# A first stage planned anew: a longer written list of steps, tile 0's root first, clamps moved off GpSimd, more tiles turned by DMA

## The chip, the cores and the metric

The kernel runs on one core of a Trainium2 chip. The metric is the device time of one execution in microseconds (us); the time of a kernel is the median of its runs. The engines are named as the profile names them: PE (TensorE), with PEld for its weight loads, DVE (VectorE), ACT (ScalarE), POOL (GpSimd) and SP (SyncE, which here only issues DMAs).

## The reference

Two graph layers, each after a layer normalisation and with a residual, over 3327 nodes of 1024 features, all in float32:

```python
# layer 0
h = jnp.maximum(_layernorm(x), 0.0)
x = x + _L0_gnn_ref(h, adj, ...)
# layer 1
h = jnp.maximum(_layernorm(x), 0.0)
x = x + _L1_gnn_ref(h, adj, ...)
```

The first layer is quantised. Its first part, which the first stage of the kernel computes, is

```python
w_norm = (weight - mean) / std
weight_q = _weight_quant(w_norm, wgt_alpha, 3)     # clip to +-1, round to 7 steps, keep the sign
x = _act_quant(input, act_alpha, 4)                # min(x / alpha, 1), round to 15 steps
support = relu(jnp.matmul(x / act_delta, weight_q / wgt_delta) * act_delta * wgt_delta)
support_q = _act_quant(support, act_alpha2, 4)
output = jnp.matmul(adj / adj_scaling_factor, support_q / support_delta)
```

so it turns 3327 x 1024 rows into small integers, multiplies them by a 1024 x 1024 matrix of small integers, and clips and rounds the result again. The product with the adjacency matrix is the second stage; the attention of the second layer and a chain of four dense layers follow.

## The kernel before

The nodes are cut into T = 26 tiles of 128 rows. The first stage makes s_int[t], one 128 x 1024 tile of integers for each t, and they stay in SBUF for the second stage.

*The weights.* The 1024 x 1024 matrix w is loaded by SP as 8 blocks of 128 rows (L347), behind the two halves of x's tile 0 (L345) and ahead of tiles 1 to 5 (L128). Mean and deviation of the weights come from statistics of each block: blocks 0 and 3 on ACT (`measure_on_scalar`, L252 to L257, a sum and a sum of squares), the other six on DVE (L364). They are joined by two small matmuls (L412, L419). Then each half block (c, k), of 128 x 512, is rounded to a byte (`round_weight`: ACT L448 or DVE L446) and clamped to +-7 into w_int (`clamp_weight`: POOL or DVE, L452). There are 16 half blocks; three of the clamps and six of the roundings are on DVE.

*One tile of rows.* A tile t passes through these steps:

- `half_stats` (bn_stats, L234, two halves) and `aggregate` (L241) on DVE give mean and variance.
- `normaliser` gives scale and bias of a pair of tiles: eps added (L271), a square root on ACT (L273), two reciprocals on DVE (L275, L280), and small arithmetic (L277, L278, L282 to L284) on POOL, or on DVE where it is given `nc.vector`. Tiles 0 and 1 have chains of their own: `half_inverse` (L133 to L136) with `scale_and_bias` (L368, L369), and the steps `first_0` to `first_3`.
- `to_bytes` (ACT, L293) normalises and rounds to bytes; `quantise` (L301, the step `clip`) clamps them to 15 as bf16 in xq, which has three buffers. They are shared with the scratch output (`junk`) of the weight statistics on ACT.
- The tile is turned so that features lie on partitions, into xqt (four buffers). Either PE does it (`transpose`, L311, eight transposes of 128 x 128, and `transposed`, ACT L314, which copies the PSUM result), or a DMA from SP (L305). `by_tensor(t)` says which: before, PE for t up to 6 and for even t.
- `products(t, c)` (L321): 8 matmuls for each of 2 column halves, accumulated in PSUM (three buffers).
- `support_bytes` (ACT, L336, the step `sum`) rounds to bytes, `support` (L339) clamps them into s_int[t].

*The order.* Nearly every instruction of the stage is pinned: each engine executes its instructions in the order in which the program writes them. The start of the stage is written out as a list of steps, the string ORDER. A step `round_0_2_v` rounds half block (0, 2) on DVE, `product_0_1_3_3` is tile 0, column half 1, k from 3 to 3, and `bytes_3` also issues the load of the pair of tiles 8 and 9. The list goes as far as the last product of tile 4. From there a loop over t takes over. Its iteration for t does, in this order: part of the normaliser of pair t // 2 + 2 (for even t), the statistics of tile t + 6, the rest of that normaliser, support of tile t - 1, bytes and clip of tile t + 3 with the load of a pair ahead of the clip, the first half of tile t's products, the turn of tile t + 2 where PE does it, and the second half. The iteration for t = 5 takes two tiles of statistics, and turns tile t + 1:

```python
            for t in range(5, T):
                ...
                if t == 5:
                    steps = normaliser(4, V)
                ...
                for u in (10, 11) if t == 5 else (t + 6,):
                ...
                ahead = t + 1 if t == 5 else t + 2
```

*The second stage* (L680) multiplies the transposed adjacency, split into a high and a low part, by s_int. Its first part is made from a load (L170) that the same loop places at t = T - 2; on SP's queue that load stands behind the last turn by DMA.

Of the kernel before, what the change touches and what calls it, by code (L numbers as in the profile page):

```python
# [8 lines left out]
F32 = mybir.dt.float32  # L9
# [6 lines left out]
ALU = mybir.AluOpType  # L16
# [4 lines left out]
P = 128  # L21
# [24 lines left out]
GT = 2  # L46
# [14 lines left out]
def two_layer_kernel(  # L61
# [101 lines left out]
    with tc.tile_pool(name="at", bufs=2, reuse_waits="tile") as atp:  # L163
# [35 lines left out]
        with tc.tile_pool(name="s1", bufs=2, reuse_waits="tile") as s1, tc.tile_pool(  # L199
# [95 lines left out]
            def by_tensor(t):  # L295
                return t % 2 == 0 or t < 7
# [10 lines left out]
            def transpose(t):  # L307
                tps[t] = tp_ps.tile([P, KF, P], BF16, name="tp")
                xq = xqs.pop(t)
                for k in range(KF):  # L310
                    pin(nc.tensor.transpose(tps[t][:, k, :], xq[:, k * P : (k + 1) * P], ident_b))  # L311
# [72 lines left out]
            next(by_act[0])  # L384
            ready[0] = scale_and_bias(half_inverse(mv0[:, 1:2], "x0", pin), mv0[:, 0:1], to_q, "x0")
            next(by_act[0])
            to_bytes(0)
            quantise(0, nc.gpsimd)
            transpose(0)
            weight_statistics(1)  # L390
# [38 lines left out]
            v1, s1_, r1, q1, b1_ = (small.tile([P, 1], F32, name=f"x1{c}", bufs=1) for c in "vsrqb")  # L429
# [24 lines left out]
            def first(i):  # L454

                if i == 0:
                    pin(nc.vector.reciprocal(r1, s1_))
                elif i == 1:
                    pin(nc.gpsimd.tensor_tensor(q1, v1, r1, ALU.mult))
                    pin(nc.gpsimd.tensor_tensor(q1, q1, s1_, ALU.add))  # L460
                elif i == 2:
                    pin(nc.vector.reciprocal(r1, q1))
                else:
                    pin(nc.gpsimd.tensor_scalar(r1, r1, to_q, -1.0, ALU.mult, ALU.mult))
                    pin(nc.gpsimd.tensor_tensor(b1_, mv1[:, 0:1], r1, ALU.mult))
                    pin(nc.gpsimd.tensor_scalar(r1, r1, -1.0, None, ALU.mult))
                    ready[1] = r1, b1_
# [8 lines left out]
            def bytes_of(t):  # L476
# [7 lines left out]
                first_0 round_0_0 round_0_2_v first_1 round_0_5_v clamp_0_2 round_0_1 first_2 clamp_0_5  # L484
                clamp_0_0_v round_0_3 round_0_6_v product_0_0_0_0 first_3 round_0_4 stats_2_0 clamp_0_1
                bytes_1 stats_3_0 clamp_0_3 product_0_0_1_2 stats_2_1 clamp_0_4 product_0_0_3_3 round_0_7
                clip_1 clamp_0_6 product_0_0_4_5 round_1_0 stats_3_1 turn_1 clamp_0_7_v product_0_0_6_6
                round_1_1 clamp_1_0 mv_2 product_0_0_7_7 mv_3 turned_1 clamp_1_1 norm_1 round_1_2_v
                round_1_5_v clamp_1_2 norm_1 product_1_0_0_0 round_1_3 product_1_0_1_1 norm_1
                product_1_0_2_2 clamp_1_5 norm_1 product_1_0_3_4 round_1_4 norm_1 product_1_0_5_5 clamp_1_3  # L490
                norm_1 product_1_0_6_6 round_1_6_v product_1_0_7_7 round_1_7 product_0_1_0_0 clamp_1_4
                product_0_1_1_2 stats_4_0 bytes_2 product_0_1_3_3 clamp_1_6 product_0_1_4_5 clamp_1_7_v
                product_0_1_6_6 stats_5_0 product_0_1_7_7 product_1_1_0_0 bytes_3 product_1_1_1_1 clip_2
                product_1_1_2_4 stats_4_1 product_1_1_5_5 sum_0 turn_2 stats_5_1 product_1_1_6_7 clip_3
                turned_2 support_0 mv_4 turn_3 mv_5 sum_1 norm_2 product_2_0_0_0 stats_6_0 product_2_0_1_3
                stats_7_0 product_2_0_4_4 norm_2 product_2_0_5_5 turned_3 product_2_0_6_6 norm_2
                product_2_0_7_7 support_1 norm_2 product_2_1_0_1 norm_2 product_2_1_2_2 norm_2
                product_2_1_3_4 stats_6_1 bytes_4 product_2_1_5_7 stats_7_1 product_3_0_0_2 mv_6 bytes_5
                product_3_0_3_3 clip_4 product_3_0_4_6 mv_7 product_3_0_7_7 product_3_1_0_0 norm_3 sum_2
                clip_5 product_3_1_1_1 turn_4 stats_8_0 product_3_1_2_3 turned_4 support_2 product_3_1_4_4  # L500
                stats_9_0 product_3_1_5_7 norm_3 stats_8_1 product_4_0_0_0 sum_3 product_4_0_1_2 norm_3
                product_4_0_3_3 norm_3 product_4_0_4_5 norm_3 product_4_0_6_6 norm_3 product_4_0_7_7
                product_4_1_0_0 support_3 stats_9_1 product_4_1_1_1 bytes_6 turn_5 mv_8 product_4_1_2_2 mv_9
                product_4_1_3_4 turned_5 product_4_1_5_6 clip_6 product_4_1_7_7 bytes_7 clip_7
# [4 lines left out]
            for step in ORDER:  # L509
# [10 lines left out]
                elif op == "support":  # L520
# [5 lines left out]
                    support(*at, nc.gpsimd)  # L526
# [12 lines left out]
            for t in range(5, T):  # L539
# [4 lines left out]
                if t == 5:  # L544
                    steps = normaliser(4, V)
                elif t % GT == 0 and pair < T // GT:
                    steps = normaliser(pair)
                for _ in range(4):
                    next(steps, None)
                for u in (10, 11) if t == 5 else (t + 6,):  # L550
                    if u < T:
                        measure(u)
# [10 lines left out]
                ahead = t + 1 if t == 5 else t + 2  # L563
                if ahead < T and by_tensor(ahead):
                    transpose(ahead)
                    transposed(ahead)
# [553 lines left out]
```

## Time and profile before

| | |
|---|---|
| median of three runs | 2250.61 us (2249.75 to 2250.79) |
| the profiled execution's own time | 2246.05 us |
| its span | 2244.1 us |
| first product of the first stage (L321) | starts at 24.41 us |
| first product of the second stage (L680) | starts at 136.12 us |
| clamps of s_int on POOL / on DVE (L339) | 4 of 2.78 us / 22 of 0.70 us |
| copies of turned tiles on ACT (L314) | 16 of 1.01 us |
| turns by DMA (L305) | 10, issue 1.23 us each |

The profile is of one execution, whose own time lies 4.6 us below the median. Times in the trace are counted from the start of its span. In a timeline a row has the start, the duration, the engine, the line and the operands, the number of instructions that it merges, and in brackets the idle time ahead of it with what ended it.

### The profile page before, as it was taken

How to read it: one execution, taken by the hardware profiler on the slowest of the kernel's cores; microseconds unless marked ns; L12 is line 12 of the kernel's file. 1: busy time of each engine (PE TensorE's matmuls, PEld its weight loads, DVE VectorE, ACT ScalarE, POOL GpSimd, SP SyncE). 2: the span in 40 equal slices, each digit the busy share in tenths (PEclk: the TensorE clock that was granted, in tenths of full speed). 3: DMA queues.
4: the chain of work that ended last, by engine and by line, in shares of the span. 5: the costliest groups of instructions: out<-in, count | busy, mean ns of one | idle time of the engine just before them, and what ended most of it. 6: DMA issues, size and time to landing. Idle time of an engine off the chain costs nothing.

```text
span 2244.1 us, 31348 instructions
## 1 busy us (share of the span) xinstructions
PE 2190.6 (98%) x12512; PEld 1747.5 (78%) x12512; DVE 1534.3 (68%) x1983; ACT 1120.3 (50%) x1690; POOL 195.2 (9%) x284
## 2 busy tenths in 40 slices
PE   4999999999999999899999999999999999999998
PEld 2467777777777777699999999999999999744444
DVE  7744555555555545578999999999999999822211
ACT  6744445544454444456556555565655555531120
POOL 4300111110111101100000000000000000000000
PEclk9999999999999999999999999999999999999999
DMA  5654666555665566844242241655242422383311
GB/s 190 163 173 144 188 179 182 157 162 174 182 180 160 153 180 182 289 156 147 78 143 86 80 132 45 224 173 155 86 147 77 144 88 78 99 208 105 111 56 56
DMA packets 236978, 320.63 MB, mean 143 GB/s; under 512 B 99796, under 2 KB 180644, under 8 KB 236832
## 3 DMA queue, kind: packets, MB, share of 16 engines
q1 hardware_dynamic: 216280, 245.45, 36.2%
q0 software_dynamic: 20544, 73.18, 10.4%
q8 instruction: 98, 1.61, 0.3%
q14 instruction: 48, 0.39, 0.1%
q10 hardware_dynamic: 8, 0.00, 0.0%
HBM read 209.25 MB, written 86.79 MB: 132 GB/s over the span
## 4 chain that ended last, share of the span: by engine, by line
PE 53%; ACT 1%; DVE 0%; DMA 0%; issue 0%; DVEq 0%
PE acc L993 27%; PE mps L786 13%; PE o L1064 8%; PE h_ps L1027 4%; ACT enct L1049 0%; PE h_ps L949 0%; DMA weights<-in_w1t 0%; ACT h L1034 0%; DVE sel L984 0%; DVE nodes L1060 0%; ACT su L830 0%; DVE su L827 0%; DVE yo L1074 0%; ACT rest L957 0%; DVEq L1117 0%
## 5 line engine op out<-in xcount | busy, mean ns | idle before, releaser
L984 DVE SCALAR_TENSOR_TENSOR sel<-srow,ndst,mask 128x896 fp32r<-128x896 f32 (+1 forms) x832 | 864.4, 1079 | 51.1 <-PE acc L993 46.0
L786 PE MATMUL mps<-dw,mf 128*128 128x260 f32 x2704 | 452.6, 283 | 0.1
L680 PE MATMUL mm<-s_int,hi 128*128 128x512 f32 x1352 | 427.2, 397 | 0.0
L680 PE MATMUL mm<-s_int,lo 128*128 128x512 f32 x1352 | 419.2, 391 | 0.0
L993 PE MATMUL acc<-f_even,sel 128*128 128x260 f32 x2704 | 398.4, 285 | 6.8 <-issue 5.1
L993 PE MATMUL acc<-f_odd,sel 128*128 128x260 f32 x2704 | 393.8, 286 | 1.0 <-ACT xs L1008 1.0
L785 ACT CAST mf<-mask 128x1664 fp32r<-128x1664 uint8 x208 | 331.5, 1594 | 112.7 <-PE mps L786 94.9
L786 PEld LDWEIGHTS mps<-dw,mf 128*128 128x128 f32 x2704 | 377.2, 188 | 0.5 <-ACT part L790 0.3
L993 PEld LDWEIGHTS acc<-f_even,sel 128*128 128x128 f32 x2704 | 355.7, 189 | 11.8 <-issue 5.9
L993 PEld LDWEIGHTS acc<-f_odd,sel 128*128 128x128 f32 x2704 | 352.6, 188 | 8.4 <-issue 2.9
L680 PEld LDWEIGHTS mm<-s_int,hi 128*128 128x128 f32 x1352 | 253.9, 188 | 63.6 <-issue 12.0
L680 PEld LDWEIGHTS mm<-s_int,lo 128*128 128x128 f32 x1352 | 252.0, 188 | 51.5
L179 DVE TENSOR_SCALAR mk<-at 128x896 uint8<-128x896 f32 (+1 forms) x104 | 61.5, 593 | 227.3 <-DMA at<-in_adj_t 227.1
L614 PE MATMUL whm<-whead,ht 128*128 128x512 f32 x416 | 184.3, 596 | 5.6 <-ACT ht L591 5.3
L1064 PE MATMUL o<-weights,h 128*128 128x512 f32 x416 | 179.7, 592 | 0.0
L1064 PEld LDWEIGHTS o<-weights,h 128*128 128x128 f32 x416 | 79.1, 190 | 99.1 <-issue 98.8
L174 ACT CAST hi<-at 128x896 fp32r<-128x896 f32 x104 | 92.5, 890 | 125.5 <-PE mm L680 85.0
L614 PEld LDWEIGHTS whm<-whead,ht 128*128 128x128 f32 x416 | 77.7, 190 | 99.2 <-issue 87.1
L855 POOL DMA_DIRECT2D enc_d<-eh x64 | 57.5, 903 | 935.0 <-ACT eh L853 875.4
L790 ACT COPY part<-mps 128x260 f32<-128x260 f32 x104 | 39.2, 377 | 194.2 <-PE mps L786 194.2
L178 DVE TENSOR_TENSOR lo<-at,hi 128x896 fp32r<-128x896 f32 x104 | 106.0, 1020 | 41.3 <-ACT hi L174 41.1
L1034 ACT ACTIVATE h<-h_ps,rest 128x512 f32<-128x512 f32 (+1 forms) x54 | 35.1, 654 | 196.1 <-PE h_ps L1027 196.1
(166 smaller groups left out, 1700.9 us busy)
## 6 DMA issues: line engine op xcount, KB each, us to landing
feat_d<-fw POOLq DMA_DIRECT2D x26, 1040.0 KB, 5.3
f_even<-feat_d SPq DMA_DIRECT2D x7, 3380.0 KB, 13.3
f_odd<-feat_d SPq DMA_DIRECT2D x7, 3380.0 KB, 12.9
at<-in_adj_t SPq DMA_DIRECT2D x52, 448.0 KB, 3.9
at<-in_adj_t SPq DMA_DIRECT2D x52, 384.0 KB, 3.6
mask<-mask_d SPq DMA_DIRECT2D x39, 416.0 KB, 7.8
dw<-dsum_d SPq DMA_DIRECT2D x16, 910.0 KB, 8.8
dsum_d<-dw POOLq DMA_DIRECT2D x26, 520.0 KB, 6.3
```

Of the source, the lines that this page charges most:

```text
L174: ins = nc.scalar.copy(hi, at)
L178: nc.vector.tensor_tensor(lo, at, hi.bitcast(F32), ALU.subtract)
L179: ins = nc.vector.tensor_scalar(mk[:, r], at, 0.0, None, ALU.is_gt)
L614: ins = nc.tensor.matmul(whm, ht[:, k, :], whead[:, k, :], start=(k == 0), stop=(k == KF - 1))
L680: nc.tensor.matmul(mm[:, c * 512 : (c + 1) * 512], which[:, q, :], s_int[j][:, c * 512 : (c + 1) * 512], start=(j == 0 and which is hi), s ...
L785: nc.scalar.copy(mf, mask[:, j : j + TH, :])
L786: nc.tensor.matmul(ps, mf[:, j % TH, :], dw[:, j, :], start=(j == 0), stop=(j == T - 1))
L855: nc.gpsimd.dma_start(enc_d[q, sub[0] * P : (sub[-1] + 1) * P, h * HD : (h + 1) * HD].rearrange("(b p) d -> p b d", p=P), eh[:, q].rearran ...
L984: nc.vector.scalar_tensor_tensor(sel[:, :nb], srow[:, :nb], ndst[:, j, h : h + 1], mask[:, :, j, :], ALU.is_gt, ALU.mult,)
L993: nc.tensor.matmul(accs[b], sel[:, b, :], f[:, j, :], start=(j == 0), stop=(j == T - 1))
L1027: nc.tensor.matmul(ps[:, :cols], wt[:, k, m * P : (m + 1) * P], xt[:, k, :cols], start=(k == 0), stop=(k == k_n - 1),)
L1064: nc.tensor.matmul(ps[:, c * 512 : (c + 1) * 512], h3[:, k, q * P : (q + 1) * P], w4[:, k, c * 512 : (c + 1) * 512], start=(k == 0), stop= ...
```

## The change

Five edits, all in the first stage. `by_tensor` names fewer tiles: 0 to 4 without gaps, then every third, where before it was 0 to 6 and then every second. The square root chain of tile 0 comes ahead of the sums of weight block 0 on ACT. Tile 1's root is computed on DVE instead of POOL (one fused multiply-add and `scale_and_bias` in place of five POOL instructions). The early supports go to DVE like all others. And ORDER is a new list that goes three tiles further, through the last product of tile 7 with everything that must be under way by then, so that the loop starts at t = 8 and the special cases for t = 5 fall away.

```diff
             def by_tensor(t):
-                return t % 2 == 0 or t < 7
+                return t % 3 == 0 or t in (1, 2, 4)
...
-            next(by_act[0])
             ready[0] = scale_and_bias(half_inverse(mv0[:, 1:2], "x0", pin), mv0[:, 0:1], to_q, "x0")
-            next(by_act[0])
             to_bytes(0)
             quantise(0, nc.gpsimd)
             transpose(0)
+            for _ in range(2):
+                next(by_act[0])
             weight_statistics(1)
...
                 elif i == 1:
-                    pin(nc.gpsimd.tensor_tensor(q1, v1, r1, ALU.mult))
-                    pin(nc.gpsimd.tensor_tensor(q1, q1, s1_, ALU.add))
+                    pin(nc.vector.scalar_tensor_tensor(q1, v1, r1, s1_, ALU.mult, ALU.add))
                 elif i == 2:
                     pin(nc.vector.reciprocal(r1, q1))
                 else:
-                    pin(nc.gpsimd.tensor_scalar(r1, r1, to_q, -1.0, ALU.mult, ALU.mult))
-                    pin(nc.gpsimd.tensor_tensor(b1_, mv1[:, 0:1], r1, ALU.mult))
-                    pin(nc.gpsimd.tensor_scalar(r1, r1, -1.0, None, ALU.mult))
-                    ready[1] = r1, b1_
+                    ready[1] = scale_and_bias(r1, mv1[:, 0:1], to_q, "x1")
...
             ORDER = """
-                first_0 round_0_0 round_0_2_v first_1 round_0_5_v clamp_0_2 round_0_1 first_2 clamp_0_5
-                clamp_0_0_v round_0_3 round_0_6_v product_0_0_0_0 first_3 round_0_4 stats_2_0 clamp_0_1
-                bytes_1 stats_3_0 clamp_0_3 product_0_0_1_2 stats_2_1 clamp_0_4 product_0_0_3_3 round_0_7
...
-                product_4_1_3_4 turned_5 product_4_1_5_6 clip_6 product_4_1_7_7 bytes_7 clip_7
+                first_0 round_0_1 first_1 first_2 first_3 round_0_0 clamp_0_1 round_0_2_v round_0_5_v
+                bytes_1 clamp_0_2 clamp_0_0_v clamp_0_5 round_0_6_v product_0_0_0_1 round_0_3
...
+                turned_4 product_3_1_4_4 stats_9_0 product_3_1_5_7 norm_3 support_0 product_4_0_0_3 norm_3
+                sum_3 product_4_0_4_4 norm_3 product_4_0_5_6 norm_3 norm_3 product_4_0_7_7 product_4_1_0_1
+                stats_8_1 bytes_6 product_4_1_2_3 stats_9_1 product_4_1_4_6 mv_8 bytes_7 product_4_1_7_7
+                clip_6 product_5_0_0_1 mv_9 product_5_0_2_2 norm_4 product_5_0_3_3 clip_7 product_5_0_4_4
...
+                norm_5 product_7_1_3_4 clip_9 bytes_10 product_7_1_5_7 support_4 turn_9 turned_9 clip_10
+                stats_12_0 stats_13_0 stats_12_1 stats_13_1 mv_12 mv_13 support_5 support_6
             """.split()
...
-                    support(*at, nc.gpsimd)
+                    support(*at)
...
-            for t in range(5, T):
+            for t in range(8, T):
...
-                if t == 5:
-                    steps = normaliser(4, V)
-                elif t % GT == 0 and pair < T // GT:
+                if t % GT == 0 and pair < T // GT:
                     steps = normaliser(pair)
...
-                for u in (10, 11) if t == 5 else (t + 6,):
-                    if u < T:
-                        measure(u)
+                if t + 6 < T:
+                    measure(t + 6)
...
-                ahead = t + 1 if t == 5 else t + 2
-                if ahead < T and by_tensor(ahead):
-                    transpose(ahead)
-                    transposed(ahead)
+                if t + 2 < T and by_tensor(t + 2):
+                    transpose(t + 2)
+                    transposed(t + 2)
```

In the new list 13 of the 16 weight clamps stay on POOL, and three (half blocks 0_0, 0_7 and 1_7) are on DVE. Beside them POOL keeps, in this stage, the clip of tile 0, a few one-column constants, and from pair 6 on the small arithmetic of the normaliser.

## The prediction

> **What bounds the kernel now.** I read the page's engine shares and slices first. TensorE (PE) is busy for 98% of the span and in every slice at nine tenths or more except the first, at four. The change touches only the first stage, so the question is what PE waits for there.
>
> ```profile
> PE 2190.6 (98%) x12512; PEld 1747.5 (78%) x12512; DVE 1534.3 (68%) x1983; ACT 1120.3 (50%) x1690; POOL 195.2 (9%) x284
> PE   4999999999999999899999999999999999999998
> ```
>
> Next the timeline of PE over the first 140 us: start, duration, work, and in brackets the idle time before it with its releaser.
>
> ```profile
> 24.41 0.58 PE L321 MATMUL mm<-w_int,xqt 128*128 128x512 bf16 x1 [3.03 <-ACT wb L448]
> 27.26 1.44 PE L321 MATMUL mm<-w_int,xqt 128*128 128x512 bf16 x3 [2.27 <-POOL w_int L452]
> ...
> 53.27 1.90 PE L321 MATMUL mm<-w_int,xqt 128*128 128x512 bf16 x8 [1.24 <-ACT xqt L314]
> ...
> 61.79 3.32 PE L321 MATMUL mm<-w_int,xqt 128*128 128x512 bf16 x8 [4.44 <-ACT xqt L314]
> 64.95 0.61 PE L311 MATMUL tp<-ident_b,xq 128*128 128x128 bf16 x8
> 65.39 7.07 PE L321 MATMUL mm<-w_int,xqt 128*128 128x512 bf16 x32
> ```
>
> The first product starts at 24.41. From 61.79 on PE never stops: the second stage's first product (L680) follows at 136.12. So whatever the first stage saves moves everything after it. Between 24.41 and the stage's last matmul end (136.47) lie 112.1 us. Its work is 416 products at 0.2158 (32 take 7.07, 8 take 1.89) = 89.8, and 15 tiles turned by PE at 0.44 (64.95 to 65.39) = 6.6. The other 15.7 us are waits (10.9 in the timeline's brackets) and matmuls at half pace. The longest wait is explained by the timelines of ScalarE (ACT) and VectorE (DVE):
>
> ```profile
> 55.31 1.10 ACT L336 ACTIVATE sb<-mm,to_s 128x1024 uint8<-128x1024 f32 x1
> 59.60 1.24 ACT L293 ACTIVATE xb<-xs,l0b,l0r 128x1024 uint8<-128x1024 f32 x1 [3.19 <-issue]
> 60.74 0.99 ACT L314 COPY xqt<-tp 128x1024 bf16<-128x1024 bf16 x1
> ```
>
> ```profile
> 57.35 1.23 DVE L234 BATCH_NORM_STATS2 stats<-xs 128x6 f32<-128x512 f32 x2
> ...
> 59.15 0.16 DVE L283 TENSOR_TENSOR l0b<-mv,l0r 128x2 f32<-128x2 f32 x1
> ```
>
> Tile 6 was turned by 55.6, but its copy out of PSUM (60.74) stands on ACT behind the bytes of tile 8, whose scale DVE finishes at 59.5, after four statistics of tiles 10 and 11. It is a fault of order at the seam where the written list ends and the loop begins (t = 5), not of load.
>
> **What the Trainium skill says.** "TensorE: Matmul & The Clock Gate", Part 1 (What's actually happening): after an idle window of about 3.4 us PE runs at half clock until it has been busy for such a window, and the window is free-running. The trace agrees: after 4.44 idle, 8 products take 3.32 instead of 1.89, and the granted clock in the stretch 60 to 70 is 0.83. Since the window is free-running, another execution need not pay this 1.4 to 1.7 us. "GPSIMD Engine Reference", 1. Specifications: GpSimd (POOL) shares its SBUF interfaces with DVE. The trace agrees: beside POOL's 2.8 us clamps the tiny scale of L284 takes up to 0.89 on DVE, alone 0.17. "DMA: Bandwidth & Descriptors", DMA Transpose (X-bar), has the plain transpose only from the Sync and Scalar queues, so the new ones share SP's queue with the row loads; here all ten run on SP, and their times to landing are:
>
> ```profile
> DMA to landing us min/median/max: 3.0/5.3/5.6
> ```
>
> Those issued within a microsecond of a pair of row loads landed after 5.1 to 5.6, two without loads ahead after 3.0.
>
> **The change part by part.** I walked both lists instruction by instruction: each starts when its engine is free, its inputs are there and its buffer is free, with durations and spacings from the groups above and handoffs of 0.03 to 0.09 us read off the timelines. For the kernel before, this gives the first product at 24.46 (trace 24.41), the long wait as 4.62 (4.44) and the stage's end at 136.02 (136.47), so I trust it to about half a microsecond where the same mechanisms rule. For the changed list it gives 24.29 and 126.29. By parts:
>
> *First root first.* x0's square root no longer stands behind the first weight block's sum on ACT, which waits until 7.6 for its load; one of two table loads (1.28) goes, since the root's table is now loaded first. Tile 0's bytes start at 7.6 instead of 11.74, POOL clips them by 11.7 instead of 16.17. DVE can begin the weight statistics when block 1 lands instead of at 11.62. But weights land one per 1.28 us (7.6, 8.9, 10.2 and so on; the loads' times to landing of 5.9 to 9.0 and the row loads waiting for them show it), block 7 at about 16.6. So the weights' mean starts at 17.9 instead of 19.15: 1.25 gained, not 4. Block 3's sum on ACT now waits for xq's buffer until PE has turned tile 0 (12.65); it ends at 15.4, ahead of 17.9, and costs nothing.
>
> *Tile 1's root on DVE.* Five tiny instructions (0.16 to 0.22 each, dependent) stand ahead of DVE's first weight rounding: about 1.0. Three POOL waits and five POOL instructions (0.19 to 0.38) go, so POOL starts its weight clamps at 22.5 instead of 23.9. All 13 clamps stay on POOL at 0.775 apart, three on DVE. Product 0 of column 1, k = 6, the last that a POOL clamp holds up, starts at 33.88 instead of 35.59: **-1.7**. By then 22 products are done in both lists, so 394 remain in both.
>
> *Fewer turns by PE.* 12 tiles instead of 16 (0 to 4, 6, 9 and so on by 3): 4 x 8 transposes off PE, 4 x 0.44 = **-1.8**, and four copies of 0.9 off ACT. Each becomes an issue of 1.23 us on SP's queue, behind the row loads (0.33 to 0.45 each). SP is idle most of the stage; its next customer is the adjacency load, which still follows the last transpose (116.6 instead of 126.57) and so stays some 4 us ahead of its use.
>
> *The seam moved from t = 5 to t = 8, the list planned anew.* POOL's four support clamps (2.78 each) and three more tiles' go to DVE at 0.63: 4 x 0.63 = 2.5 us more on DVE, which has 6.0 us idle between 35 and 62 in the walk of before, and no POOL work stretches its tiny instructions there. In the new walk DVE idles 5.1 there, but only 0.4 of 14 us between 62 and 76, where its supports meet the loop's first statistics. PE's waits after 34 become 0.72 (tile 5, the first turned by DMA), 0.16 (tile 8), 1.29 (the turn of tile 12, behind DVE's clip) and 0.84 (tile 11): 3.0. Before, they were 1.11 + 0.38 + 1.24 + 4.44 = 7.2, with 0.17 of pipeline end at each, and 1.6 of half clock: 9.5. **-6.5**.
>
> Sum: -1.7 - 1.8 - 6.5 = **-10.0**, or -9.7 walk against walk. Against the profiled execution's own 2246.05 that is 2236. The median of the runs, 2250.61, lies 4.6 higher; I take the difference as holding for it, less 0.8 for half of the half-clock time that not every run pays: -9.0, so **2241.6 us**. The second stage starts with the same 26 tiles and the same loads in the same order, all about 10 us earlier; later stages are untouched.
>
> Unknown costs. A DMA transpose behind loads when two follow within 3.45 us: at 4.5 us the walk ends at 124.3, at 5.4 at 125.9, at 6.5 at 128.1, at 7.5 at 130.5 (last matmul starts, against 135.6 before). I take 5.4, the median behind loads. DVE's instructions 10% slower, which would bite at 62 to 76: 128.0, as 20% slower ACT gives 129.4; the lower bound is no slowdown, since nothing there gets shorter.
>
> **Rivals.**
> *Transposes crowd the queue.* Seven in ten of the loop's tiles now turn by DMA, beside 1 MB of rows every two tiles. Against it: a 256 KB transpose moved at a mean DMA share of 0.24 in the stretch 110 to 120. At 6.5 to 7.5 us to landing the gain is 7.4 to 5.1, less 0.8: 2243 to 2246.5.
>
> *DVE becomes the bound where the seam now lies.* For it: it is full from 62 to 76. If its instructions run 20% longer there and earlier, the end is 131.3, a gain of 4.3, less 0.8: about 2247, within what can be told from no change.
>
> *Slower: late transposes put PE to sleep.* Place: tiles 5 and 11, the two products that wait for a DMA turn. Up to 8.5 us to landing the walk still ends at 133.5, ahead of before. From about 8.6 on these waits pass 4 us, each costs a half-clock window besides, and the end jumps to 138.4 at 9 us and 141.4 at 10: +2.8 to +5.8, that is 2253.4 to 2256.4. Against it: no landing above 5.6 in this trace.
>
> *It doesn't do what it says.* The compiled lists exclude that: PE's has 64 rows fewer (32 weight loads, 32 transposes), POOL's has no support clamps, one table load is gone.
>
> **How the numbers follow.** Main case, gain 6 to 11: 0.70, its own range 2239.5 to 2244.5. Crowded queue: 0.12. DVE bound: 0.11. Slower: 0.07. A difference of 0.2%, 4.5 us, is about what a measurement can tell from none. Faster by more (below 2246.1): 0.70 and most of the crowded case, 0.81. Same: 0.12. Slower: 0.07. The range reaches from 2238.5 (landing at 4.5 and all half-clock time saved) to 2246.5 (landing at 7.5).
>
> **What would show it.** Right: the first L680 matmul at 126 to 127; 12 tiles turned by PE; no wait of PE over 2 us after 25; no drop of the granted clock between 30 and 130; transposes landing within 6 us; the first L452 on POOL near 22.5. Wrong: PE waiting for the xqt of tiles 5, 8 or 11 for over 3 us, or DVE late with clips at 60 to 76 and PE's wait named after xq; or a second stage whose first product waits for hi or lo.

## The result and the profile after

The changed kernel takes **2240.67 us** (median of five, 2240.19 to 2241.67) against 2250.61 (2249.38 to 2251.28) for the kernel before in the same rounds: a ratio of 0.9957, with a 95% interval of 0.9943 to 0.9972, or 9.9 us less. Forecast were 2241.6 us and a range of 2238.5 to 2246.5. Ratios below are to the kernel before, with a 95% interval.

The page of the changed kernel, the shares and PE's slices:

```profile
PE 2190.0 (98%) x12470; PEld 1747.2 (78%) x12480; DVE 1536.8 (69%) x1996; ACT 1114.9 (50%) x1685; POOL 180.4 (8%) x269
...
PE   5999999999999999899999999999999999999998
```

The totals hardly move. The first slice goes from four tenths to five, but a second trace of the kernel before (e1) has five there too, so the slices can't tell. PE's timeline of the changed kernel shows where the waits now are:

```profile
24.74 1.44 PE L321 MATMUL mm<-w_int,xqt 128*128 128x512 bf16 x3 [4.51 <-DVE w_int L452]
...
33.65 0.38 PE L321 MATMUL mm<-w_int,xqt 128*128 128x512 bf16 x1 [0.56 <-POOL w_int L452]
34.40 1.70 PE L321 MATMUL mm<-w_int,xqt 128*128 128x512 bf16 x4 [0.37 <-POOL w_int L452]
...
50.52 2.33 PE L321 MATMUL mm<-w_int,xqt 128*128 128x512 bf16 x10 [0.43 <-DMA xqt<-xq]
...
71.84 0.62 PE L311 MATMUL tp<-ident_b,xq 128*128 128x128 bf16 x8 [1.26 <-DVE xq L301]
...
75.00 8.81 PE L321 MATMUL mm<-w_int,xqt 128*128 128x512 bf16 x39 [0.82 <-DMA xqt<-xq]
...
128.41 0.82 PE L680 MATMUL mm<-s_int,hi 128*128 128x512 f32 x2
```

Where the kernel before stood 4.44 us for a copy on ACT, the longest wait after the first product is now 1.26. The second stage (L680) starts at 128.41 instead of 136.12.

The profiled executions differ by less than the medians: 2246.05 against 2241.67, 4.4 us. The rest of the program, from the first L680 to the end of the span, took 2244.1 - 136.12 = 2108.0 us in the first profile of the kernel before, and between 2109 and 2115 in each of the thirteen others taken here. So that profile had the shortest remainder of all. One difference is in the granted clock: behind the second stage, between 930 and 951, every trace has a stretch at 0.50, which is 3.4 us long in that profile, 6.8 in eight of the others and 10.2 in five. The first stage is therefore better judged by where L680 starts.

### The profile page after: what moved, and what is told of

Its sections match the earlier page's. It is cut to its first block, busy times and chain, and to the rows that moved or that the text cites. A ratio compares the mean times of both kernels' runs of the same rounds, so it can differ in the third digit from the quotient of the medians.

```text
span 2239.9 us, 31268 instructions
## 1 busy us (share of the span) xinstructions
PE 2190.0 (98%) x12470; PEld 1747.2 (78%) x12480; DVE 1536.8 (69%) x1996; ACT 1114.9 (50%) x1685; POOL 180.4 (8%) x269
## 4 chain that ended last, share of the span: by engine, by line
PE 53%; ACT 1%; DVE 0%; DMA 0%; issue 0%; DVEq 0%
PE acc L993 27%; PE mps L786 13%; PE o L1064 8%; PE h_ps L1027 4%; ACT enct L1049 0%; PE h_ps L949 0%; DMA weights<-in_w1t 0%; ACT h L1034 0%; DVE sel L984 0%; DVE nodes L1060 0%; ACT su L830 0%; DVE su L827 0%; DVE yo L1074 0%; ACT rest L957 0%; DVEq L1117 0%
## 5 line engine op out<-in xcount | busy, mean ns | idle before, releaser
L680 PE MATMUL mm<-s_int,hi 128*128 128x512 f32 x1352 | 427.2, 397 | 0.0
L680 PE MATMUL mm<-s_int,lo 128*128 128x512 f32 x1352 | 419.1, 391 | 0.0
L680 PEld LDWEIGHTS mm<-s_int,hi 128*128 128x128 f32 x1352 | 253.9, 188 | 63.6 <-issue 12.0
L680 PEld LDWEIGHTS mm<-s_int,lo 128*128 128x128 f32 x1352 | 252.0, 188 | 51.4
```

The lines of the kernel that those rows point to most:

```text
L680: nc.tensor.matmul(mm[:, c * 512 : (c + 1) * 512], which[:, q, :], s_int[j][:, c * 512 : (c + 1) * 512], start=(j == 0 and which is hi), s ...
```

## The experiments

All kernels, ordered by what they tell. L410 is the start of the weights' mean.

| kernel | median us | ratio (95%) | L410 | first L680 |
|---|---|---|---|---|
| before, first trace | 2250.61 | | 19.15 | 136.12 |
| e1: before again | 2250.20 | 1.0003 (0.9994 to 1.0011) | 19.36 | 137.22 |
| changed, first trace | 2240.67 | 0.9957 (0.9943 to 0.9972) | 17.99 | 128.41 |
| e5: changed again | 2240.60 | 0.9958 (0.9945 to 0.9970) | 17.94 | 126.40 |
| e2: before, two of three tiles by DMA | 2248.21 | 0.9996 (0.9988 to 1.0005) | 19.40 | 135.30 |
| e3: before, tile 6 turned earlier | 2246.77 | 0.9987 (0.9981 to 0.9994) | 18.54 | 132.21 |
| e4: before, both start edits | 2248.03 | 0.9995 (0.9987 to 1.0003) | 18.92 | 134.01 |
| e9: before, all of these, old list | 2240.46 | 0.9958 (0.9944 to 0.9972) | 17.65 | 126.33 |
| e11: changed, root behind the weight sum | 2241.11 | 0.9964 (0.9952 to 0.9977) | 19.10 | 127.81 |
| e6: changed, early supports on POOL | 2242.63 | 0.9968 (0.9958 to 0.9978) | 17.92 | 128.07 |
| e7: changed, transposes behind a copy | 2247.17 | 0.9991 (0.9985 to 0.9998) | 18.34 | 135.46 |
| e8: changed, waits filled with matmuls | 2237.73 | 0.9948 (0.9935 to 0.9960) | 18.10 | 126.81 |
| e12: the kernel of e8 again | 2238.99 | 0.9952 (0.9939 to 0.9966) | 17.10 | 126.17 |
| e10: e8, six steps moved | 2237.76 | 0.9949 (0.9937 to 0.9962) | 17.84 | 126.07 |

The last two columns come from one execution each, and three of these lie well off their kernel's median: e3's took 2244.41 us, the second shortest of its runs, e4's 2250.73, the longest, and e7's 2250.95, the second longest.

### Both kernels again (e1, e5)

> The kernel before once more, unchanged, for a second trace of it on the chip on which the next three run. The profiled execution of before had 2246.05 us where its timed runs had 2250.61. If the difference is one of execution to execution, this trace has its first stage end near 136.1 us again (within 0.5; up to 1.7 less if the half clock after the long wait is not paid this time) and the difference lies in later stages, in PE's waits of the second stage for the turned tile ht (L614) and in half-clock windows. If the first stage itself varies from execution to execution by several us, then the gain of the change can't be read from single traces. Ratio to before: 1.000.

> The changed kernel once more, unchanged, for a second trace and a fresh comparison with the kernel before. In its first trace PE ran at half clock from 35.2 to 38.6 us although no wait there was longer than 0.6 us, and the second stage started at 128.41 where the walk had 126.3. If the half-clock window belongs to the kernel's short waits for weight clamps at 31.8 to 35.2, it can be here again or not, as its windows run free: second stage at 126.5 to 127 without it, at 128.4 with it. If instead the walk mis-sized a wait, the start is at 128.4 again with no half clock in the trace. Ratio to before 0.9945 to 0.997.

The second trace of the kernel before has its long wait at the same place, again followed by half pace, 3.59 us for eight products:

```profile
62.01 3.59 PE L321 MATMUL mm<-w_int,xqt 128*128 128x512 bf16 x8 [4.45 <-ACT xqt L314]
```

It starts L680 1.1 us later than the first trace, more than the 0.5 that was expected: 0.2 of it is there at the first product, and the rest is half clock, which lasts 6.8 us here (59.9 to 66.7) instead of 3.4.

Its remainder is 2248.6 - 137.22 = 2111.4, that of e5 2239.1 - 126.40 = 2112.7 and that of the first trace of the changed kernel 2111.5. Between e1 and e5 the second stage comes 10.8 us earlier, between the two first traces 7.7, and the medians differ by 9.9 in the first rounds and by 8.8 in those of e5 (2249.40 for the kernel before). PE's timeline of e5:

```profile
34.35 1.02 PE L321 MATMUL mm<-w_int,xqt 128*128 128x512 bf16 x4 [0.37 <-POOL w_int L452]
...
70.23 0.62 PE L311 MATMUL tp<-ident_b,xq 128*128 128x128 bf16 x8 [1.26 <-DVE xq L301]
...
72.99 8.81 PE L321 MATMUL mm<-w_int,xqt 128*128 128x512 bf16 x39 [0.41 <-DMA xqt<-xq]
```

It is 2.01 us ahead of the first trace at L680. The wait for tile 5 (0.43 there) is gone and that for tile 11 is 0.41 shorter; the other 1.2 us lie between 34.4 and 38.7, where the first trace ran four products in 1.70 instead of 1.02. That is half clock (see e8).

### One edit at a time (e2, e3, e4)

e2, fewer turns by PE:

```diff
-                return t % 2 == 0 or t < 7
+                return t % 3 == 0 or t < 7
```

> The kernel before with one line changed: by_tensor names t % 3 == 0 or t < 7, so that in the loop two of three tiles are turned by DMA (7, 8, 10, 11, ...) and one by PE, 13 turns by PE instead of 16. Theory (a PE turn costs 0.44 us of a PE that never stops there, a DMA turn is hidden): the first product of the second stage starts 3 x 0.44 = 1.3 us earlier, at 134.8, and the transposes land within 6 us. Rival (the transposes crowd the queue of the row loads): landing over 6.5 us, PE waits for xqt of tiles 8 or 11, and the second stage starts no earlier or later than 136.1.

L680 starts at 135.30. The interval holds 1, so the edit alone isn't resolved by time. The trace still has half clock at 62.3 to 65.7: with the long wait left in place, transposes saved elsewhere are worth little more than themselves.

e3, the one fault of order that the forecast named:

```diff
-                product_4_1_3_4 turned_5 product_4_1_5_6 clip_6 product_4_1_7_7 bytes_7 clip_7
+                product_4_1_3_4 turned_5 product_4_1_5_6 clip_6 product_4_1_7_7 bytes_7 clip_7 turn_6 turned_6
...
-                if ahead < T and by_tensor(ahead):
+                if ahead in xqs and ahead < T and by_tensor(ahead):
```

> The kernel before with only the turn of tile 6 and its copy moved to the end of the written list, ahead of the loop's iteration for t = 5, so that the copy no longer stands on ACT behind the bytes of tile 8. Theory (the 4.44 us wait is a fault of order at the seam, not of load): the copy runs near 54, PE does not wait for xqt of tile 6, and the second stage starts 3 to 4 us earlier, at 132 to 133: the wait of 4.4 and its half clock (1.7) go, but a new wait of about 2.9 follows one tile later, at the turn of tile 8, whose bytes still wait for DVE's normaliser behind the statistics of tiles 10 and 11. Rival (load: DVE and ACT can't deliver tile 8 sooner and PE merely waits elsewhere for the same time): the wait reappears whole before tile 7 or 8, and the second stage starts within 1 us of 136.1.

This one step gains 0.13% (0.06 to 0.19), and L680 starts at 132.21, as expected; about 0.6 us of that is an earlier start of this execution (L410 at 18.54). The half clock behind the long wait is gone too. ACT's copy of tile 6 moves from 60.74 to 53.66, ahead of the bytes of tile 8. ACT's row, and then PE's, of e3:

```profile
53.66 1.00 ACT L314 COPY xqt<-tp 128x1024 bf16<-128x1024 bf16 x1
```

```profile
52.71 0.62 PE L311 MATMUL tp<-ident_b,xq 128*128 128x128 bf16 x8 [1.28 <-DVE xq L301]
...
61.03 0.62 PE L311 MATMUL tp<-ident_b,xq 128*128 128x128 bf16 x8 [2.52 <-DVE xq L301]
```

Of 4.44 us, 2.52 come back one turn later: PE now waits for the clip of tile 8. That wait had been hidden behind the longer one.

e4, both edits of the start: the roots of tiles 0 and 1 as in the change, everything else as before.

```diff
-            next(by_act[0])
             ready[0] = scale_and_bias(half_inverse(mv0[:, 1:2], "x0", pin), mv0[:, 0:1], to_q, "x0")
-            next(by_act[0])
...
+            for _ in range(2):
+                next(by_act[0])
...
-                    pin(nc.gpsimd.tensor_tensor(q1, v1, r1, ALU.mult))
-                    pin(nc.gpsimd.tensor_tensor(q1, q1, s1_, ALU.add))
+                    pin(nc.vector.scalar_tensor_tensor(q1, v1, r1, s1_, ALU.mult, ALU.add))
...
-                    ready[1] = r1, b1_
+                    ready[1] = scale_and_bias(r1, mv1[:, 0:1], to_q, "x1")
```

> The kernel before with the two edits of the start alone: tile 0's root ahead of the weight parts on ACT, and tile 1's root on DVE. Old list otherwise, supports on POOL, turns as before. Theory: the weights' landing sets the gain; the weights' mean (L410) starts at 17.9 to 18.0 instead of 19.15, POOL's first weight clamp at 22.8 or earlier instead of 23.9, the last product that a clamp of POOL holds up at 33.6 to 34.0 instead of 35.6, and the second stage starts 1.7 us earlier, at 134.4. Rival A (the root was the bound, not the landing): the mean starts at 15 to 16 and the second stage 3 to 4 us earlier. Rival B (the gain is lost again, as DVE now delays the weight roundings): first product no earlier than 24.4 and the second stage within 0.5 us of 136.1.

The second stage starts at 134.01, but the time isn't resolved from none. In this execution the second weight block landed about 1 us later (DVE waited 2.83 us for it), so its mean started at 18.92 only.

### All edits but the list (e9)

The three kernels above put together, with supports on DVE (`support(*at)`); the old list, but for `turn_6 turned_6` at its end, and the old loop from t = 5 on.

> The kernel before with its old list and its loop from t = 5, and in it the four small edits together: both roots first, the four early supports on DVE, two of three loop tiles turned by DMA (13 by PE), the turn of tile 6 and its copy at the end of the list. What the change has beyond it is the new order itself, three tiles of list more, and tile 5 turned by DMA. Theory by the walk (127.25 against 125.9 for the change and 135.6 for before): the parts add up to most of the gain, and the second stage starts at 127.5 to 128.5, about 1.4 us later than in the change without its half clock (126.4); waits of 0.5 before tile 7 and 1.8 before the turn of tile 9 remain. Rival (the new order is the gain; the small edits only shift a wait, as the single ones did): the second stage starts at 130 or later, with a wait of over 3 us in the iterations for t = 6 to 8. Ratio to before 0.9955 to 0.9975 by the theory, 0.998 or more by the rival.

It equals the change: 2240.46, 0.9958 (0.9944 to 0.9972), L680 at 126.33, 1 to 2 us earlier than expected. PE's timeline of e9, the waits that are left:

```profile
48.70 0.62 PE L311 MATMUL tp<-ident_b,xq 128*128 128x128 bf16 x8 [0.52 <-DVE xq L301]
...
59.94 0.62 PE L311 MATMUL tp<-ident_b,xq 128*128 128x128 bf16 x8 [1.70 <-DVE xq L301]
```

In e3 PE waited 1.28 at the turn of tile 6 and 2.52 at that of tile 8; here tile 8 is turned by DMA, and 0.52 (tile 6) and 1.70 (tile 9) are left. Two things follow. The newly planned list with its seam moved to t = 8 brings nothing measurable over the old one with one turn moved. And the parts seem to be worth more together: against the kernel before in their rounds (2249.08) the medians of e2, e3 and e4 gain 0.9 + 2.3 + 1.1 = 4.3 us, e9 with the supports besides gains 9.3 (from 2249.74). At L680, counted from the mean of the two traces of before (136.67), it is 1.4 + 4.5 + 2.7 = 8.6 against 10.3. The intervals of the single edits are wide, and L410 alone varies from 18.54 to 19.40 among the four traces with the old start, so that the whole exceeds the sum isn't shown, and which part would do it wasn't separated.

### The start, undone (e11)

The changed kernel with tile 0's root put back behind the sum of weight block 0; tile 1's root stays on DVE.

```diff
+            next(by_act[0])
             ready[0] = scale_and_bias(half_inverse(mv0[:, 1:2], "x0", pin), mv0[:, 0:1], to_q, "x0")
+            next(by_act[0])
...
-            for _ in range(2):
-                next(by_act[0])
```

> The changed kernel with tile 0's root back behind the sum of weight block 0 on ACT, as before; all else as changed. Theory (the start is worth what the weights' landing leaves: 1.2 to 1.3 us): the weights' mean (L410) starts at 19.2 instead of 17.9, the first product at 25.9 instead of 24.7, and the second stage 1.3 us later than in the change, at 127.7 (129.4 with a half-clock window at 33 to 40). Rival (later waits absorb it, since POOL's clamps and DVE bound what follows): less than 0.4 us later.

All three marks came as expected: L410 at 19.10, L680 at 127.81, 1.4 later than in e5, and the first product, in PE's timeline of e11:

```profile
25.85 1.44 PE L321 MATMUL mm<-w_int,xqt 128*128 128x512 bf16 x3 [4.52 <-DVE w_int L452]
```

By time it is 0.5 us slower than the changed kernel, and the intervals overlap: shown in the trace, not by the clock of the runs. The reason is in the changed kernel's rows, of ACT and then DVE:

```profile
6.29 0.20 ACT L133 ACTIVATE x0s<-mv 128x1 f32<-128x1 f32 x1 [2.89 <-DVE mv L383]
7.61 1.24 ACT L293 ACTIVATE xb<-xs,x0b,x0r 128x1024 uint8<-128x1024 f32 x1 [1.12 <-DVE x0b L369]
```

```profile
12.76 5.13 DVE L364 BATCH_NORM_STATS2 w_stats<-w 128x6 f32<-128x512 f32 x8 [1.18 <-DMA w<-in_w]
17.99 0.51 DVE L410 BATCH_NORM_AGGREGATE w_mv<-w_stats 128x2 f32<-128x78 f32 x1
```

The root is done by 6.5 and the bytes start at 7.61, so DVE is free to follow the weights as they land; at 12.76 it still waits for one, and the mean follows right on the last.

### Early supports on POOL (e6)

```diff
-                    support(*at)
+                    support(*at, nc.gpsimd)
```

> The changed kernel with the seven supports of its list (tiles 0 to 6) on POOL again; everything else as changed. Theory by the walk (POOL is idle from 34 to 65, DVE is full from 62 to 76): DVE is relieved by 7 x 0.63 us, the waits before the turn of tile 12 and the product of tile 11 shrink by about 0.5 in all, and the second stage starts 0.5 us earlier than in the change as it stands. Rival (POOL's 2.8 us clamps take the port that DVE's tiny instructions need, as beside them L284 took 0.89 instead of 0.17): the normaliser chains of pairs 4 and 5 stretch by 1 to 3 us each, bytes and turns come late, and the second stage starts 1 to 4 us later than in the change; then moving the supports off POOL is part of the gain.

It lands at 128.07, 1.7 later than e5, and in time 0.10% over it with overlapping intervals. The walk had this variant 0.5 earlier, so the rival was right in the trace. First POOL's row of e6, then DVE's rows under it, then the same two lines on DVE in e5:

```profile
45.36 5.62 POOL L339 TENSOR_SCALAR s_int<-sb 128x1024 fp32r<-128x1024 uint8 x2 [3.56 <-ACT sb L336]
```

```profile
47.11 1.04 DVE L282 TENSOR_SCALAR l0r<-l0r,to_q 128x2 f32<-128x2 f32 x1
...
48.38 0.89 DVE L284 TENSOR_SCALAR l0r<-l0r 128x2 f32<-128x2 f32 x1
```

```profile
46.12 0.23 DVE L282 TENSOR_SCALAR l0r<-l0r,to_q 128x2 f32<-128x2 f32 x1
...
46.57 0.17 DVE L284 TENSOR_SCALAR l0r<-l0r 128x2 f32<-128x2 f32 x1
```

The two instructions of one normaliser take 1.93 beside POOL instead of 0.40. That agrees with the shared SBUF interfaces of the Trainium skill ("GPSIMD Engine Reference", 1. Specifications): 0.69 us of DVE work moved to POOL does not free 0.69 us of DVE.

### Later transposes (e7)

A 512 KB copy from DRAM to DRAM, of data that nothing uses, is issued ahead of each transpose by DMA.

```diff
                 if not by_tensor(t):
-                    nc.sync.dma_start_transpose(xqts[t], xqs.pop(t))
+                    pin(nc.sync.dma_start(spare_d[t], w0[:P, :]))
+                    pin(nc.sync.dma_start_transpose(xqts[t], xqs.pop(t)))
```

> The changed kernel with a copy of 512 KB from DRAM to DRAM put on SP's queue ahead of each of the 14 DMA transposes; the copied data are used nowhere. It makes the transposes land later, to find what the change can bear. Theory by the walk: landing grows by 1.3 us or more (one copy's time on the 16 DMA engines) from 5.4 to about 6.7 behind loads and from 3.0 to 4.3 without; PE's waits for tiles 5 and 11 grow from 0.4 and 0.8 to about 2.4 and 2.1, a wait for tile 10 appears, and the second stage starts 2.6 us (if a copy costs 1.3) to 5 us (if it costs 2.0) later than in the change. Rival (the transposes have slack everywhere and the waits named after them come from DVE): less than 1 us later, with landing over 6.5. Other rival (a transpose does not tolerate other traffic): landing over 9 us, PE waits of over 4 us, half clock, 8 us or more.

Times to landing, first of the changed kernel, then of e7:

```profile
DMA to landing us min/median/max: 3.0/4.9/5.6
```

```profile
DMA to landing us min/median/max: 3.0/5.7/8.3
```

PE's waits for them in e7 (its lines stand two further down):

```profile
52.81 2.33 PE L323 MATMUL mm<-w_int,xqt 128*128 128x512 bf16 x10 [2.27 <-DMA xqt<-xq]
...
78.86 4.03 PE L323 MATMUL mm<-w_int,xqt 128*128 128x512 bf16 x11 [2.37 <-DMA xqt<-xq]
...
103.66 8.81 PE L323 MATMUL mm<-w_int,xqt 128*128 128x512 bf16 x40 [1.55 <-DMA xqt<-xq]
```

The waits for tiles 5 and 11 came where and about as long as foreseen, the third, for tile 17, was not foreseen, and neither was the total: L680 at 135.46 is 9.1 later than in e5. Of this, 0.4 is there at the first product (25.08 against 24.69), where no transpose plays a part. The three waits are 6.2 us against 0.4, which is 5.8. The other 2.9 is half clock: the trace has two stretches of it, 35.4 to 38.8 and 79.8 to 83.2 (granted 0.50), and e5 has none there. From the product at 34.74 to the turn at 39.13, e7 takes 1.3 more than e5 does from 34.35 to 37.46, and from the product at 78.86 to the turn at 89.19 1.7 more than e5 from 72.99 to 81.64. The second stretch follows one in which PE was busy 1.03 of 3.4 us, with 2.37 as its longest wait, so half clock can follow shorter waits than the 4 us I had put as its point; after the wait of 2.27 it didn't come. The profiled execution is one of the slowest, and by the medians e7 loses 6.6 us to e5. That is still most of the change's gain, which therefore hangs on transposes that land in time.

### Filled waits (e8, e12), and six steps moved (e10)

In e8 PE does eight more matmuls, two each ahead of four products of tile 0 that wait for weight clamps. Their results are not used.

```diff
-                product_0_1_3_3 clamp_1_7_v bytes_2 clamp_1_5 product_0_1_4_4 stats_4_0 clamp_1_6
+                fill_2 product_0_1_3_3 clamp_1_7_v bytes_2 clamp_1_5 fill_2 product_0_1_4_4 stats_4_0 clamp_1_6
-                product_0_1_5_5 stats_5_0 bytes_3 clip_2 product_0_1_6_7 product_1_1_0_0 stats_4_1
+                fill_2 product_0_1_5_5 stats_5_0 bytes_3 clip_2 fill_2 product_0_1_6_7 product_1_1_0_0 stats_4_1
...
+            def fill(n):
...
+                        nc.tensor.matmul(
+                            mms[2][:, :512], xqts[1][:, 0, :], w_int[:, 0, :512], start=True, stop=True
+                        )
```

> The changed kernel with 8 extra matmuls of 128x512 on PE, two ahead of each of the products of tile 0, column 1, k = 3, 4, 5 and 6, into the PSUM tile that tile 2's products later overwrite; they compute nothing that is used. They fill the short waits for POOL's weight clamps at 31.8 to 35.2. Theory (a window with PE busy only about half of the time, without one long wait, is enough for the half clock that the first trace of the change shows at 35.2 to 38.6): no half clock after 31 us in this trace, and the second stage starts 1.5 to 2 us earlier than in the first trace of the change (128.4), at 126.4 to 127, though 8 x 0.22 = 1.7 us of work are added. Rival (the half clock has nothing to do with these waits): the half clock is there again, or the added matmuls delay the products and the second stage starts at 128.4 or later.

> The changed kernel with the eight fills once more, unchanged, for a second trace and a fresh comparison. Theory (the fills keep PE's clock up in every execution, where the change pays a half-clock window of 1.5 to 2 us in some): ratio to before 0.994 to 0.9955 again, no half clock between 30 and 40 us, second stage at 126.4 to 127. Rival (the lower median of the first such run was a matter of the later stages): a median within 1 us of the change's two (2240.6 and 2240.7), that is a ratio of 0.9955 to 0.9965.

Is it true that short waits bring half clock? The traces let the stretch ahead of a half clock be placed. Every stretch at 0.50, but for some at the very end of the span, lasts 3.41 us or two or three times that, and within one trace they start whole numbers of such steps apart: 34.60 and 935.72 in the first trace of the changed kernel are 264 steps of 3.413, and 35.38, 79.76 and 939.92 in e7 are 13 and 252. So there is a grid of steps that runs through the whole execution. The program doesn't set its place: a step ends at 34.60 in the first trace and at 33.47 in e5, of the same program. The rows below are steps of it, with start and end, length, busy time of PE, PEld, DVE, ACT and POOL with counts, granted clock, DMA share, GB/s. First the one ahead of the half clock in the first trace of the changed kernel, and the half clock itself:

```profile
31.20:34.60 3.40, 1.71 (x5) 0.48 (x5) 3.33 (x8) 2.64 (x4) 2.83 (x5) 1.00 0.00 0
34.60:38.00 3.40, 3.18 (x14) 1.69 (x14) 3.37 (x9) 2.62 (x3) 0.00 (x0) 0.50 0.52 166
```

Then e7, one step that was followed by half clock and one that wasn't:

```profile
31.97:35.38 3.41, 1.78 (x7) 0.57 (x6) 3.34 (x8) 2.64 (x4) 2.48 (x4) 1.00 0.00 0
49.04:52.45 3.41, 1.51 (x7) 0.49 (x5) 3.06 (x11) 1.98 (x3) 0.00 (x0) 1.00 0.94 197
```

In e5 the grid, counted back from the half clock at 931.18, divides the same short waits between two steps:

```profile
30.06:33.47 3.41, 2.87 (x13) 1.14 (x12) 3.24 (x10) 2.65 (x4) 3.09 (x5) 1.00 0.00 0
33.47:36.88 3.41, 2.55 (x16) 1.24 (x17) 3.41 (x7) 3.17 (x4) 0.75 (x2) 1.00 0.22 56
```

And e8, a stretch that holds most of the fills (not a step of its grid):

```profile
31.80:35.20 3.40, 3.35 (x17) 1.47 (x16) 3.33 (x8) 2.64 (x4) 2.42 (x4) 1.00 0.00 0
```

So half clock did come after a step in which PE was busy half of the time and never waited more than 0.6 us, and the place of the grid fits the difference between two executions of one program. A limit can't be read from this: 1.71 and 1.78 us (5 and 7 matmuls) were followed by half clock, 1.51 in e7, 1.57 in e3 (from 56.94), 1.72 in e9 (from 57.90) and 1.85 in e11 (from 33.46), with 7, 8, 15 and 8 matmuls, were not. Of the changed kernel and its variants without fills, two of five traces have half clock in this place (the first and e7, but not e5, e6 and e11), with fills none of three (e8, e10, e12). That fits the expectation and is too little to show it.

The fills make eight matmuls more and cost nothing: 2237.73 and 2238.99 us. In the rounds that e5 and e8 share, four of the five times of e8 (2237.10 to 2239.47) lie below the lowest of e5 (2239.31). The ratios' intervals overlap, so about 0.1% of gain is likely and not settled. The reason isn't settled either: e5 had no half clock in the first stage, L680 of e8 starts no earlier than that of e5, and its lead of 3.1 us in that trace lies in the remainder, where the half clock behind the second stage is 6.8 us long in e8 and 10.2 in e5.

e10 moves six steps of e8's list forward, to have the clip of tile 12 in time:

```diff
-                product_5_1_7_7 product_6_0_0_0 stats_11_0 product_6_0_1_3 support_2 product_6_0_4_4 sum_4
+                product_5_1_7_7 product_6_0_0_0 stats_11_0 product_6_0_1_3 support_2 stats_12_0 stats_13_0 product_6_0_4_4 sum_4
...
-                mv_11 product_7_0_2_2 norm_5 product_7_0_3_3 support_3 product_7_0_4_4 norm_5
-                product_7_0_5_6 norm_5 sum_6 product_7_0_7_7 norm_5 product_7_1_0_1 norm_5 product_7_1_2_2
+                mv_11 stats_12_1 product_7_0_2_2 norm_5 product_7_0_3_3 support_3 product_7_0_4_4 norm_5
+                product_7_0_5_6 norm_5 sum_6 product_7_0_7_7 norm_5 mv_12 product_7_1_0_1 norm_5 product_7_1_2_2
```

The other two are `stats_13_1`, put ahead of `product_7_1_3_4`, and `support_1`, ahead of `product_4_0_7_7`.

> The changed kernel with the fills of the short waits as in the run before (8 extra matmuls that compute nothing used), and six steps of the list moved to earlier places: the statistics of tiles 12 and 13 (four halves and one mean), from the end of the list into the products of tiles 6 and 7, and support_1 into those of tile 4. Theory (DVE is full from 62 to 76 because the list leaves the statistics of tiles 12 and 13 and two supports to its end, and idle before): the waits before the turn of tile 12 (1.27) and the product of tile 11 (0.4 to 0.8) go, and the second stage starts 1.5 to 2 us earlier than in the change without its half clock, at 124.6 to 125.2; ratio to before 0.993 to 0.9945. Rival (the row loads of tiles 12 and 13 are not there that early, so that DVE waits for them and delays all behind): DVE waits for xs at 52 to 56, and the second stage starts at 126.8 or later.

The turn of tile 12 no longer waits, but L680 at 126.07 is 0.1 to 0.7 ahead of e12 and e8, not the 1 us and more that was expected. DVE's row of e10, then PE's:

```profile
54.38 0.69 DVE L234 BATCH_NORM_STATS2 stats<-xs 128x6 f32<-128x512 f32 x1 [0.63 <-DMA xs<-in_x]
```

```profile
60.89 0.62 PE L311 MATMUL tp<-ident_b,xq 128*128 128x128 bf16 x8 [1.02 <-DVE xq L301]
```

Statistics put earlier now wait for their rows, and the clip of tile 9 comes late in their stead: 1.26 at one turn became 1.02 at another. At 2237.76 it doesn't differ from e8. Best of all kernels run are e8, e10 and e12.

## Why the prediction was right, step by step

**The whole.** The walk put L680 at 126.29; it came at 128.41 and 126.40. The forecast gain of 9.0 was measured as 9.9 and, in e5's rounds, as 8.8. By L680 the two pairs of traces give 7.7 and 10.8, 9.3 in the mean. That the sum is right to within 1 us is in part luck: in e5 the start came 0.5 later than walked and the waits behind it were 0.5 shorter. The discount of 0.8 was for executions of the kernel before that don't pay the half clock. None of these was seen: all four traces that have the wait of 4.4 (before, e1, e2 and e4) have half clock behind it, while of two traces of the changed kernel one had half clock in another place, which the walk didn't have. Some sums of the prediction don't come out, none of which decides: by its own walk the range should begin at 2239.3 (a gain of 11.3 holds the half clock already), the crowded case at 2244.0 instead of 2243, and of the loop's tiles two in three are turned by DMA.

**First root first** held: L410 at 17.99 (forecast 17.9), one table load, the gain set by the landing of the weights. e11 prices it at 1.1 to 1.4, as the 1.25 forecast.

**Tile 1's root on DVE**, where the start's -1.7 was summed, was mis-sized. POOL's first clamp came at 22.59 (forecast 22.5), but the first product at 24.74 instead of 24.29, and the last one held by a clamp at 34.40 and 34.35 instead of 33.88. So -1.7 was -1.2. The walk priced DVE's first weight clamp, which the first product waits for, at 0.41; it took twice that. DVE's timeline of the changed kernel, then of the kernel before:

```profile
23.86 0.83 DVE L452 TENSOR_SCALAR w_int<-wb 128x512 bf16<-128x512 int8 x1
```

```profile
23.95 0.41 DVE L452 TENSOR_SCALAR w_int<-wb 128x512 bf16<-128x512 int8 x1
```

Why isn't shown. POOL was clamping at that time in both (from 23.57 and from 23.92), so POOL's work alone doesn't explain it.

**Fewer turns by PE**: 12 copies of turned tiles on ACT instead of 16, as forecast. The price of -1.8 fits e2's 135.30 (0.8 and 1.9 below the two traces of before), but no run isolates it.

**The seam.** The waits after 34, forecast at 3.0 (0.72, 0.16, 1.29, 0.84), were 0.43, none, 1.26 and 0.82, 2.5 in sum, or 3.0 with the 0.17 of pipeline end at each that the walk seems to hold (it has 4.62 for the 4.44 of the trace). In e5 they were 2.0, or 2.5, with a turn at 35.67 that waited 0.30. The size was right, the credit too wide: the step ascribes 6.5 to the seam moved and the list planned anew, and e9 gets the same with the old list, one turn moved and the other edits. What e3 shows is a row of waits behind one another, of which a trace shows only the longest.

**No drop of the clock between 30 and 130** was wrong in the first trace (34.6 to 38.0) and right in the second. No wait ahead of it exceeds 0.6 us. "TensorE: Matmul & The Clock Gate", Part 1, of the Trainium skill names an idle window as what puts PE to half clock; here the step ahead of it was busy for half of its length, and the measurement decides. That the windows run free, as the prediction has it from the same part, agrees with the grid of steps at e8.

**The rivals.** Crowded queue: transposes landed in 3.0 to 5.6, like before. e7 shows the mechanism as real and, in its trace, dearer than its price: the walk had its end at 133.5 for 8.5 us to landing, and with 8.3 at most and 5.7 in the median L680 came at 135.46. The walk gave half clock only to waits over 4 us, and e7 had one of its two half clocks after a wait of 2.37. What the slower rival needs therefore begins earlier than 8.6 us, though e7 was still not slower than before. DVE as the bound: it is nearly full where forecast, idle for 1.2 of 14 us between 62 and 76 (0.4 in the walk), and what it costs is the 1.26 at tile 12. e10 tried to take that away and mostly moved it.

## What to carry to other kernels

A trace shows the longest of several waits that stand behind one another, so a fault taken away alone returns only the difference to the next one (1.9 of 4.44 us in e3, besides the half clock), and edits of 0.9 and 1.1 us, not resolved singly, were part of one of 9.3. Before planning a whole list anew, move the one step that the longest wait names and try it with the cheap edits around it: that gave all of the gain here. Where a stage hangs on transfers that just land in time, test with a load beside them how steep the loss is.

## What was not expected of the hardware

The clock fell to half after a step of 3.41 us in which PE was busy 1.71 and never waited more than 0.6, and in e7 after 1.78, but not after 1.51 in the same trace; the same program did both in two executions. Each half clock of the first stage cost 1.2 to 1.7 us where it could be told. Two small instructions on DVE grew from 0.17 to 0.89 and from 0.23 to 1.04 us beside a clamp on POOL (e6). A 128x512 clamp on DVE took 0.41 or 0.83, for a reason that no run shows.
